# Two linear-attention layers: the key products of two jobs made by the same matmuls

## The chip, the cores and the metric

The kernel runs on one core of a Trainium2 chip. The metric is the device time of one execution in microseconds; the time before is the median of three runs. The profiled execution is a further one, and its time and its span are given below.

## The reference

The input x has 32 sequences of 128 tokens with 512 features, in float32. Two layers follow each other, with 16 heads in the first and 8 in the second; each is, for one sequence (`mask`, `cond`, weights and biases given):

```
xn = layernorm(x) * s + b
q, k, v = xn @ Wq + bq, xn @ Wk + bk, xn @ Wv + bv      # 512 x 512 each
k[masked tokens] = -inf (layer 0) or -1e6 (layer 1);  v[masked tokens] = 0
q = softmax(q, over the features of a head)
k = softmax(k, over the 128 tokens)
y = q @ (k.T @ v)                                       # head by head
h = layernorm(y) * (1 + scale(cond)) + shift(cond)      # FiLM, from silu(cond) @ We
x = x + silu(h) @ Wo + bo
```

## The kernel before

**Jobs.** Two sequences are a job; 16 jobs in a layer make 32 jobs, 0 to 31. `job()` writes out a job's operations: load and normalise (z), transpose by DVE and a round trip over DRAM (`zb`, `zd`), scale into `xnT` (features on partitions) on ACT, keys, q and v, softmaxes, attention (`pa`, `py`), second norm, transposes (`yb`, `yd`) and Silu into `hT`, output products (`oa` to `oe`), and the store. Job 0 (`plain`) multiplies directly. The last job transposes on TensorE (`xtp`, `htp`) and makes its output products (`op`) directly too, storing four pieces of 128 KB; every other job stores 512 KB at once.

**Seven products.** In jobs 1 to 31 the product of (2 sequences) x (2 halves of the features) with (2 x 2 quarters of a weight) is made of seven products of blocks in place of eight. `sums()` makes four sums of token blocks on POOL (`Sx`, L615), `sum_w` those of the weights. For the keys the stationary operand is a quarter of the weight and the moving one a block of tokens, so that a matmul moves 128 columns (one sequence); for q, v and the output the tokens are stationary, and 512 or 256 columns move. A float32 matmul leaves two records in the profile. A product of the keys is four matmuls, eight records (L743). The first product of a PSUM bank is copied out with the bias by ACT (`kcopy`, L749), two later products are added into the same bank, and the other banks are added in SBUF by DVE (`kadd`, L754):

```python
kprod(1, Ak); kcopy(0, 0); kprod(2, Bk); kadd(0, 0, Bk)
kprod(6, Ak, False); kcopy(0, 1); kprod(4, Ck)
...
```

After that the mask is added on POOL (L788), the maximum taken on DVE (L791), exp on ACT (L795), the keys of layer 0 scaled on POOL (L800), and transposed.

**Buffers.** `xnT`, `Sx` and `kT` have two buffers of a job each. All eight PSUM banks are shared. The film weights `we` have one buffer; a film group is 16 small matmuls (`em`, L546) behind a load of 1 MB.

**Order.** Each operation is recorded with `op(place, engine, estimated time, function, reads, writes, due=...)`. A planner (`Plan.schedule`) then lists them: at each step it takes the engine that can start first and, on it, the operation with the earliest due time. The due time is the job's base (31 us a job) plus the `due` of the call plus an entry of the table `SHIFT`, which holds a shift for each place and stage; `LATER` does this for loads, and `SAFE` is a margin for results of another engine. Each engine runs its list in order and waits on semaphores.

## Time and profile before

| | us |
|---|---|
| median of 3 runs (lowest, highest) | 915.11 (914.37, 915.85) |
| profiled execution, own time | 916.37 |
| its span on the core | 914.6 |
| TensorE (PE) busy in the span | 900.1 |
| VectorE (DVE) busy | 775.1 |
| ScalarE (ACT) busy | 625.2 |
| GpSimd (POOL) busy | 530.9 |

Busy times of matmuls overlap a little, so that what a matmul costs is read from the distance between the starts of two that follow each other. In a line of the timeline stand start, length, engine, line of the code, operation, output and inputs, shape and number; what ended an idle stretch before it is in brackets. In a line of a stretch the length comes first, then the busy time and number of instructions of PE, its weight loads, DVE, ACT and POOL, the granted clock, the share of DMA and its rate.

### The profile page before, as it was taken

How to read it: one execution, taken by the hardware profiler on the slowest of the kernel's cores; microseconds unless marked ns; L12 is line 12 of the kernel's file. 1: busy time of each engine (PE TensorE's matmuls, PEld its weight loads, DVE VectorE, ACT ScalarE, POOL GpSimd, SP SyncE). 2: the span in 40 equal slices, each digit the busy share in tenths (PEclk: the TensorE clock that was granted, in tenths of full speed). 3: DMA queues.
4: the chain of work that ended last, by engine and by line, in shares of the span. 5: the costliest groups of instructions: out<-in, count | busy, mean ns of one | idle time of the engine just before them, and what ended most of it. 6: DMA issues, size and time to landing. Idle time of an engine off the chain costs nothing.

```text
span 914.6 us, 18770 instructions
## 1 busy us (share of the span) xinstructions
PE 900.1 (98%) x6438; PEld 638.7 (70%) x6438; DVE 775.1 (85%) x1628; ACT 625.2 (68%) x1562; POOL 530.9 (58%) x737
## 2 busy tenths in 40 slices
PE   6999999999999999999999999999999999999998
PEld 2657567777776777766776866776777776776766
DVE  4778998879797898889999799898988997889775
ACT  3544857777867778588496757887478776666853
POOL 2465637677745778567555564654556664466543
PEclk9999999999999999999999999999999999999999
DMA  7588989595888676887969758656868465665742
GB/s 223 164 251 241 275 244 316 179 281 184 243 272 251 192 258 211 258 254 216 288 207 275 218 159 260 200 199 205 253 211 258 163 212 194 214 190 173 225 144 93
DMA packets 129891, 202.50 MB, mean 221 GB/s; under 512 B 13699, under 2 KB 81539, under 8 KB 129797
## 3 DMA queue, kind: packets, MB, share of 16 engines
q1 hardware_dynamic: 129796, 201.31, 71.0%
q8 instruction: 51, 0.84, 0.4%
q14 instruction: 44, 0.35, 0.1%
HBM read 120.00 MB, written 81.26 MB: 220 GB/s over the span
## 4 chain that ended last, share of the span: by engine, by line
PE 95%; DMA 3%; ACT 1%; DVE 1%; SPq 0%; issue 0%; ACTq 0%
PE bank_qa L817 17%; PE bank_qe L817 11%; PE bank_ka L743 9%; PE bank_oa L1013 9%; PE bank_py L946 6%; PE bank_ke L743 6%; PE bank_oe L1013 6%; PE bank_qc L817 6%; PE bank_qb L817 5%; PE bank_kc L743 3%; PE bank_oc L1013 3%; PE bank_ob L1013 3%; PE bank_kb L743 3%; PE bank_pa L925 3%; PE bank_qp L832 2%; DMA we<-in_We_dram 2%
## 5 line engine op out<-in xcount | busy, mean ns | idle before, releaser
L795 ACT ACTIVATE kT<-kT,kmax 128x128 f32<-128x128 f32 x256 | 99.8, 391 | 54.6 <-DVE kmax L791 52.5
L858 POOL TENSOR_TENSOR q<-q,qmax 128x512 f32<-128x512 f32 x64 | 67.1, 1051 | 118.1 <-DVE qmax L857 115.2
L749 ACT ACTIVATE kT<-bank_ka,cols_c 128x128 f32<-128x128 f32 x248 | 76.6, 362 | 86.2 <-PE bank_ka L743 84.5
L788 POOL TENSOR_TENSOR kT<-kT,mb 128x512 f32<-128x512 f32 x64 | 81.9, 1280 | 71.7 <-DVE kT L754 55.4
L817 PE MATMUL bank_qa<-wqv,Sx 128*128 128x512 f32 x248 | 117.3, 595 | 1.6 <-DVE v L821 1.4
L817 PE MATMUL bank_qe<-wqv,Sx 128*128 128x512 f32 x248 | 116.8, 593 | 0.0
L977 ACT ACTIVATE hT<-yb,fc_c,fa_c 128x128 f32<-128x128 f32 x248 | 102.5, 483 | 0.4
L817 PEld LDWEIGHTS bank_qa<-wqv,Sx 128*128 128x128 f32 x248 | 44.6, 190 | 42.4 <-issue 36.6
L946 PEld LDWEIGHTS bank_py<-att_c,qT 128*128 128x128 f32 x512 | 64.4, 192 | 13.4 <-issue 11.1
L743 PEld LDWEIGHTS bank_ka<-Sx,wk 128*128 128x128 f32 x496 | 63.6, 192 | 14.3 <-issue 11.2
L615 POOL TENSOR_TENSOR Sx<-xnT 128x256 f32<-128x256 f32 x62 | 46.4, 757 | 46.1 <-PE bank_qe L817 23.9
L743 PEld LDWEIGHTS bank_ke<-Sx,wk 128*128 128x128 f32 x496 | 63.2, 192 | 12.7 <-issue 10.2
L817 PEld LDWEIGHTS bank_qe<-wqv,Sx 128*128 128x128 f32 x248 | 44.6, 190 | 39.1 <-issue 37.0
L695 ACT ACTIVATE xnT<-zb,cols_c 128x256 f32<-128x256 f32 x120 | 64.0, 591 | 6.5 <-PE bank_qc L817 6.5
L657 ACT ACTIVATE y<-y,nmrb,rstdb 128x512 f32<-128x512 f32 x60 | 47.0, 809 | 29.3 <-POOL nmrb L645 29.2
L946 PE MATMUL bank_py<-att_c,qT 128*128 128x128 f32 x512 | 66.2, 275 | 0.4 <-DVE att_c L934 0.4
L743 PE MATMUL bank_ka<-Sx,wk 128*128 128x128 f32 x496 | 65.9, 276 | 0.0
L743 PE MATMUL bank_ke<-Sx,wk 128*128 128x128 f32 x496 | 65.5, 276 | 0.0
L1013 PE MATMUL bank_oa<-wo,Sh 128*128 128x256 f32 x248 | 64.2, 382 | 0.1
L1013 PE MATMUL bank_oe<-wo,Sh 128*128 128x256 f32 x248 | 64.2, 382 | 0.0
L657 ACT ACTIVATE z<-z,nmra,rstda 128x512 f32<-128x512 f32 x60 | 47.0, 807 | 18.2 <-POOL nmra L645 17.6
L817 PE MATMUL bank_qc<-wqv,xnT 128*128 128x512 f32 x124 | 58.6, 595 | 0.0
(144 smaller groups left out, 2246.6 us busy)
## 6 DMA issues: line engine op xcount, KB each, us to landing
x<-x SPq DMA_DIRECT2D x32, 512.0 KB, 4.2
qd<-qb SPq DMA_DIRECT2D x31, 512.0 KB, 4.1
qb<-qd SPq DMA_DIRECT2D x124, 128.0 KB, 3.8
kd<-k SPq DMA_DIRECT2D x31, 512.0 KB, 4.3
k<-kd SPq DMA_DIRECT2D x124, 128.0 KB, 3.7
yd<-yb SPq DMA_DIRECT2D x31, 512.0 KB, 3.9
yb<-yd SPq DMA_DIRECT2D x124, 128.0 KB, 3.7
zd<-zb SPq DMA_DIRECT2D x30, 512.0 KB, 4.7
```

What stands on the lines that cost most here:

```text
L615: op(25, "POOL", pool(2 * T), lambda i=i, x=x, y=y, f=f: nc.gpsimd.tensor_tensor(S.ap[:, i], x(), y(), f), r, [(S, i)], due=due, lock=True)
L657: op(34, "ACT", act(512, 2, False), lambda: nc.scalar.activation(dst.ap[:, b, :], src.ap[:, b, :], AF.Identity, bias=nmr.ap[:, b : b + 1], ...
L695: op(39, "ACT", act(GT, 2, False), lambda c=c: nc.scalar.activation(xnT.ap[:, c, :].rearrange("p (b r t) -> p r b t", b=G, r=4), zb.ap[:, ...
L743: nc.tensor.matmul(t.ap[:, m * T : (m + 1) * T], kw[quarter].ap[:, c, m * P : (m + 1) * P], a()[:, c, :], start=(first and m == 0 and c == ...
L749: op(46, "ACT", act(T, 1), lambda m=m: nc.scalar.activation(kT.ap[:, 2 * h + m, i, :], Ak.ap[:, m * T : (m + 1) * T], AF.Identity, bias=co ...
L788: op(50, "POOL", pool(2 * GT), lambda hs_=hs_: nc.gpsimd.tensor_tensor(kT.ap[:, hs_].rearrange("p m b t -> p m (b t)"), kT.ap[:, hs_].rear ...
L795: op(52, "ACT", act(T, 1, False) + 0.093, lambda m=m, b=b: nc.scalar.activation(kT.ap[:, m, b, :], kT.ap[:, m, b, :], AF.Exp, bias=km.ap[: ...
L817: nc.tensor.matmul(t.ap, a()[:, c, :], wqv[quarter].ap[:, c, :], start=(first and c == 0), stop=(c == 1), skip_group_check=not first)
L858: op(61, "POOL", pool(512, False), lambda qh=qh, qm=qm: nc.gpsimd.tensor_tensor(qh(), qh(), qm.ap[:, :H].unsqueeze(2).to_broadcast([P, H, ...
L946: nc.tensor.matmul(py.ap[:, m * P : (m + 1) * P], qTc(b, m), att.ap[:, b, m, :], start=True, stop=True)
L977: op(81, "ACT", act(T, 2, False), lambda c=c, b=b: nc.scalar.activation(hT.ap[:, c, b * T : (b + 1) * T].rearrange("p (r t) -> p r t", r=4 ...
L1013: nc.tensor.matmul(t.ap[:, :hf], a()[:, c, :], ow[quarter].ap[:, c, :], start=(first and c == 0), stop=(c == 1), skip_group_check=not first)
```

## The change

The keys of two jobs (four sequences) are made by the same products. The jobs 2 and 3, 4 and 5, to 28 and 29 are 14 pairs; 1, 30 and 31 stay alone, and job 0 is as before. `job` becomes a generator that stops before the keys; a new function `keys` then records the key products for one job or two. A product of a pair still has four matmuls, and each moves 256 columns, two pieces of 128 that lie a slot apart. Tokens (`xnT`), token sums (`Sx`) and keys (`kT`) of two jobs lie in one tile each, with a slot for even and one for odd jobs, and are allocated once. A copy of ACT takes 256 columns and an addition of DVE 512 elements. Everything else of a job is as before.

The tables `SHIFT` and `LATER` are new throughout, and `SAFE` has other margins, so that the order of the instructions is another on every engine. In it, job 0's key products stand ahead of its q and v products, the first film groups come earlier, and at the end job 30's output products and its store come after job 31's. Loads of activation tables on ACT number 77, before 59.

```diff
-    SAFE = {"PE": 0.62, "DVE": 0.21, "ACT": 0.52, "POOL": 0.22, "SP": 4.38}
+    SAFE = {"PE": 0.77, "DVE": 0.16, "ACT": 0.55, "POOL": 0.30, "SP": 5.07}
...
-    k_xnT = kind("xnT", [P, NC, GT], 2)
-    k_S = {s: kind("S" + s, [P, 4, 2, T], 2) for s in "xh"}
-    k_kT = kind("kT", [P, NC, G, T], 2)
+    xnT2 = fixed("xnT", [P, NC, 2, GT])
+    Sx2 = fixed("Sx", [P, 4, 2, 2, T])
+    kT2 = fixed("kT", [P, NC, 2, G, T])
+    k_Sh = kind("Sh", [P, 4, 2, T], 2)
...
+    def keys(j, L, lefts):
+        n = f"{j}_{L}"
+        kw = W["k", L]
+        J = len(lefts)
+        at = slice(j % 2, j % 2 + J)
+        Ak, Bk, Ck, Ek = (bank.new(f"k{c}{n}") for c in "abce")
+        out_ = lambda t: t.ap[:, : J * GT].rearrange("p (m j t) -> p m j t", m=2, j=J)
...
+        def prod(i, t, first=True, due=5):
+            _, _, quarter, where = lefts[0][i]
+            made = [x for l in lefts for x in l[i][1]]
+            def moving(c):
+                if isinstance(where, tuple):
+                    return xnT2.ap[:, 2 * where[1] + c, at, where[0] * T : (where[0] + 1) * T]
+                return Sx2.ap[:, where, c, at]
+            def go():
+                for m in range(2):
+                    for c in range(2):
+                        nc.tensor.matmul(out_(t)[:, m], kw[quarter].ap[:, c, m * P : (m + 1) * P], moving(c),
+                                         start=(first and m == 0 and c == 0), stop=(c == 1), skip_group_check=True)
+            op(35, "PE", mm(4, J * T), go, made + [kw[quarter]], [t], due=due)
+        def copy(i, h, due=5):
+            for m in range(2):
+                op(36, "ACT", act(J * T, 1), lambda m=m: nc.scalar.activation(
+                    kT2.ap[:, 2 * h + m, at, i, :], out_(Ak)[:, m], AF.Identity, bias=col(L, C_BK + 2 * h + m)),
+                    [Ak, cols_sb], parts(i, h, [m]), due=due)
+        def add(i, h, t, due=6):
+            op(37, "DVE", dve(J * GT), lambda: nc.vector.tensor_tensor(
+                kT2.ap[:, 2 * h : 2 * h + 2, at, i, :], kT2.ap[:, 2 * h : 2 * h + 2, at, i, :], out_(t), ALU.add),
+                [t], parts(i, h, range(2)), due=due)
...
-        kT, km, ks = k_kT.new(n), k_km.new(n), k_ks.new(n)
+        km, ks = k_km.new(n), k_ks.new(n)
+        kT = lambda: kT2.ap[:, :, slot]
+        yield left
...
+    FIRST = [i for i in range(2, 2 * B // G - 2, 2)]
+    jobs, lefts = {}, {}
...
-        job(j, L, FAR(i), i in (0, 2 * B // G - 1), i == 0)
+        jobs[i] = job(j, L, FAR(i), i in (0, 2 * B // G - 1), i == 0)
+        lefts[i] = next(jobs[i])
+        if i in FIRST:
+            continue
+        pair = [i - 1, i] if i - 1 in FIRST else [i]
+        plan.base = pair[0] * STEP
+        if i:
+            keys(pair[0] % (B // G), L, [lefts[q] for q in pair])
+        for q in pair:
+            plan.base = q * STEP
+            for _ in jobs[q]:
+                pass
```

## The prediction

> **What bounds the kernel now.** I read the page first, then the stretches, then single matmuls.

> ```profile
> PE 900.1 (98%) x6438; PEld 638.7 (70%) x6438; DVE 775.1 (85%) x1628; ACT 625.2 (68%) x1562; POOL 530.9 (58%) x737
> ...
> PEclk9999999999999999999999999999999999999999
> ...
> PE 95%; DMA 3%; ACT 1%; DVE 1%; SPq 0%; issue 0%; ACTq 0%
> ```

> TensorE is busy nearly all the time at full clock, and the chain that ended last is made of its matmuls. The stretches say where it is not:

> ```profile
> 115.00:450.00 335.00, 335.00 (x2496) 240.33 (x2495) 291.97 (x622) 246.38 (x615) 215.12 (x298) 1.00 0.78 242
> 450.00:850.00 400.00, 400.00 (x2851) 287.69 (x2850) 354.41 (x747) 280.96 (x701) 226.20 (x313) 1.00 0.68 213
> ```

> The first figure after the length is PE: 335.00 of 335 and 400.00 of 400 us. In the middle 735 us only less matmul time can help. The timeline of PE gives the price of a matmul as the distance between starts (durations overlap):

> ```profile
> 306.36 1.03 PE L1013 MATMUL bank_oa<-wo,hT 128*128 128x256 f32 x4
> 307.22 1.03 PE L1013 MATMUL bank_oc<-wo,hT 128*128 128x256 f32 x4
> ...
> 319.37 1.05 PE L743 MATMUL bank_ke<-Sx,wk 128*128 128x128 f32 x8
> 320.26 1.06 PE L743 MATMUL bank_kc<-xnT,wk 128*128 128x128 f32 x8
> 321.15 1.06 PE L743 MATMUL bank_kb<-xnT,wk 128*128 128x128 f32 x8
> 322.05 1.88 PE L817 MATMUL bank_qe<-wqv,Sx 128*128 128x512 f32 x4
> ```

> A key product (8 records of 128 columns) takes 0.895 us, 111.9 ns a record; four records of 256 columns take 0.86 us, 215.5 ns a record. The ends are where PE waits:

> ```profile
> 16.55 9.30 PE L832 MATMUL bank_qp<-wqv,xnT 128*128 128x512 f32 x16 [1.03 <-ACT xnT L712]
> 25.68 7.07 PE L763 MATMUL bank_kp<-xnT,wk 128*128 128x256 f32 x32
> ...
> 65.23 1.98 PE L817 MATMUL bank_qb<-wqv,xnT 128*128 128x512 f32 x4
> 68.43 1.08 PE L546 MATMUL bank_em<-we,cT_c 128*32 128x128 f32 x32 [1.22 <-DMA we<-in_We_dram]
> ```

> ```profile
> 108.44 1.43 PE L743 MATMUL bank_kc<-xnT,wk 128*128 128x128 f32 x8 [0.70 <-ACT xnT L695]
> ```

> ```profile
> 895.03 1.13 PE L946 MATMUL bank_py<-att_c,qT 128*128 128x128 f32 x8 [0.39 <-DVE att_c L934]
> ...
> 896.87 1.05 PE L946 MATMUL bank_py<-att_c,qT 128*128 128x128 f32 x8
> ...
> 901.38 0.66 PE L966 MATMUL bank_htp<-ident_c,y 128*128 128x128 f32 x4
> ```

> ```profile
> 911.34 0.48 DVE L998 SCALAR_TENSOR_TENSOR x<-x,nanf_c,bank_op 128x256 f32<-128x256 f32 x1 [1.25 <-PE bank_op L995]
> ```

> ```profile
> we<-in_We_dram SPq DMA_DIRECT2D x8, 1024.0 KB, 7.2
> ...
> out_dram<-x SPq DMA_DIRECT2D x15, 512.0 KB, 3.6
> ...
> out_dram<-x SPq DMA_DIRECT2D x4, 128.0 KB, 1.8
> ```

> **Part 1, the key products.** 14 pairs (jobs 2 to 29) make 98 products of 8 records with 256 columns, at 8 x 0.2155 = 1.724 us, in place of 196 at 0.895. Each pair of products gives 2 x 0.895 - 1.724 = 0.066 us, in all 98 x 0.066 = **-6.5 us**. Jobs 1, 30 and 31 stay single. [...] The rows say 2 x 111.9 - 215.5 = 8.3 ns a record, and I take the rows. No row shows a moving operand of two pieces of 128 columns; from below nothing, from above the two 128-column records' own time (gain 0). I take the contiguous price, as the 256-column rows of L763 and L1013 agree (25.68 to 32.59 is 32 x 0.216).

> **Part 2, copies and adds.** ACT: 224 copies of 128 columns (L749, 362 ns mean) become 112 of 256 (L766 does that form in 474): -28 us busy. DVE: 112 adds at 0.41 become 56 of 512 columns, for which L824 takes 0.68: -8 us. The new order carries 77 table loads for 59: 18 x 1.283 = +23 us on ACT. [...]

> **Part 3, waits in the middle.** xnT, Sx and kT become single tiles of two slots. The waits that the new program carries are by slot and part, so a write to one slot doesn't wait for a reader of the other. New is that the pair's first key product waits for the second job's tokens. I summed PE's work, by the rows above, between the last product that reads a slot's old tokens and the first that needs its new ones, where four ACT writes of 0.59 must fit: for second jobs 2.6 us at the least (pair 22/23), then 6.9, median 14; before, the least was 2.6 as well (four jobs of 32), median 11, without a stall. From the last q/v product to the job's first attention product: least 3.5, median 20 (before 1.8 and 10). From a product to the next into the same q bank: least 0.86, then 1.72, against 0.0 and 1.0 before, where the wait of 1.40 near 104 us sits. So the new order is looser, and I charge 0.

> **Part 4, the head.** Before: 1.03 at 16.55; 16 records of 0.43 took 9.13 instead of 6.88, so 2.25; 1.5 before 68.43; about 3.3 from 102 to 109 (1.40, 0.70 and what surrounds them): 8.1 us lost. After: the key matmuls of job 0 stand first (6.9 us from about 15.5, weights loaded early), then Q's 6.9 to 29.3: 3.3 us won. But the first film group (`em`) and a q product now follow. That product needs job 1's tokens, whose ACT writes stand behind the exp of q: q add 0.7, max 0.7, subtraction 1.05, exp 0.63 after 29.3, then the writes: 33.2; PE waits 2.6. The film weights have one buffer: the second load starts when the first group ends (31), takes 7.2, and one product of 1.72 us covers it: PE waits 3.3, to 38.5. In all 5.9 for 8.1: **-2.2**, and I use -2.

> **Part 5, the tail.** Job 31 is the last, and its chain from py through the norm to `htp` (transposes), Silu and `op` (output products) has no work of its own to hide it. Before, four groups of job 30's output products fill PE between the second py and the first `htp` (897.8 to 901.38), and PE does not wait. In the new order both `htp` groups stand right behind py, and job 30's output products come after them. From the end of the first py (before: 896.16): y 0.65, stats 0.65, another add 0.4, aggregate 0.15, POOL 0.25+0.6, the norm 0.55 with the second y and stats ahead of it on DVE: first `htp` 4.0, second 5.0 after py, where the order leaves 1.8; then four Silus of 0.36 before the first `op`. PE loses 3.0 there. Behind it 0.2 (Silus of job 30) and 0.5 (the last product waits for an add), 3.7 in all where before lost 0.5: +3.2. A v add stuck behind eight exps on DVE's queue holds PE 1.6 before that, against 1.2: +0.4. Last comes job 30's output: one DMA of 512 KB (3.6) instead of 128 KB (1.8): +1.8. Sum **+5.4**.

> **The sum.** -6.5 - 2 + 5.4 = -3.1 against the profiled execution: span 914.6, own time 916.37, so 913.3. The median of the runs lies 1.26 lower (915.11): 912.0. The measurement can tell about 0.2%, 1.8 us, from no change.

> **Rivals.**
> A, the sum above: 912.0, 909.5 to 914. For it: a full PE and unchanged matmuls. Chance 0.50.
> B, the tail costs little, since DVE and ACT come earlier than I string them up: -6.5 - 2 + 1.8 = -6.7, 908.4 (906 to 909.5). Against it: the `htp` groups stand where they stand. 0.15.
> [...]
> D, slower: the pair's first key product waits for the second job's tokens. The row at 108.44 is that wait, 0.70. Once for each pair: 14 x 0.7 = 9.8, 921.8. It decides from 3.1 / 14 = 0.22 us a pair, and is measurably slower from 0.35 (917). For it: the keys of two jobs come in one burst, so ACT, which must write the tokens, gets eight copies and 16 exps close together. Against it: the median of 14 us. 0.20, the lower prices likelier.

> **Numbers.** Faster by over 0.2% (below 913.3): 0.45 of A and all of B: 0.60. Within: 0.05 of A, 0.13 of C, 0.04 of D: 0.22. Slower (above 916.9): 0.02 of C, 0.16 of D: 0.18. The range 907.0 to 918.0 leaves out the best of B and the dear part of D; A and B alone hold 906.5 to 914.

> **What would show it.** Right: the pair's products start 1.72 us apart where nothing stands between; PE 735 of 735 us in the middle; gaps before the second film group near 33 to 38 us and before `htp` and the first `op`, some 3 us each; the last DMA is 512 KB. Wrong: a pair product at 1.79 or more (C); a wait on ACT's xnT before L683 in most pairs (D); no gap at `htp` (B).

## The result, and the profile after

| | before | after |
|---|---|---|
| median, us | 914.99 (914.37 to 915.85, 4 runs) | 931.05 (929.87 to 931.89, 4 runs) |
| profiled execution, own time | 916.37 (shown above) | 931.89 |
| its span | 914.6 | 930.1 |

The change makes the kernel slower by 16.1 us: the ratio is 1.0174, with a 95% interval from 1.0156 to 1.0192. The forecast was 912.0, from 907 to 918.

The page of the changed kernel, with the same parts as shown before:

```profile
PE 902.0 (97%) x5654; PEld 614.3 (66%) x5654; DVE 769.0 (83%) x1572; ACT 630.7 (68%) x1468; POOL 537.5 (58%) x737
...
PEclk9999999999999999999999999999999999999997
...
PE 88%; DVE 5%; ACT 2%; DMA 2%; issue 1%; SPq 1%; POOL 0%; ACTq 0%; POOLq 0%
```

PE has fewer records (5654, before 6438), and its share of the chain that ended last fell from 95% to 88%. The stretches say where it lost; first the two ends of the kernel before, then the changed kernel:

```profile
0.00:115.00 115.00, 104.30 (x690) 64.69 (x691) 85.56 (x172) 61.13 (x164) 59.05 (x87) 1.00 0.79 232
850.00:915.00 65.00, 60.77 (x407) 46.00 (x405) 43.14 (x91) 36.70 (x83) 30.54 (x40) 1.00 0.44 143
```

```profile
0.00:115.00 115.00, 101.26 (x620) 60.67 (x621) 78.19 (x151) 49.11 (x121) 52.06 (x74) 0.97 0.78 240
115.00:450.00 335.00, 330.10 (x2056) 223.66 (x2055) 285.14 (x597) 254.97 (x596) 218.05 (x301) 1.00 0.77 232
450.00:850.00 400.00, 398.43 (x2539) 276.64 (x2538) 354.02 (x717) 289.33 (x671) 234.48 (x322) 1.00 0.70 216
850.00:931.00 81.00, 72.16 (x443) 53.38 (x441) 51.64 (x109) 37.34 (x83) 32.92 (x43) 0.94 0.40 133
```

The middle from 450 us on is nearly full. The two ends are not, and the granted clock (the figure behind POOL) is 0.97 and 0.94 there, where the kernel before shows 1.00. PE's timeline at the first end:

```profile
16.08 8.93 PE L802 MATMUL bank_kp<-xnT_c,wk 128*128 128x256 f32 x32
24.84 7.03 PE L854 MATMUL bank_qp<-wqv,xnT_c 128*128 128x512 f32 x16
31.80 1.08 PE L547 MATMUL bank_em<-we,cT_c 128*32 128x128 f32 x32
35.66 3.02 PE L839 MATMUL bank_qb<-wqv,xnT_c 128*128 128x512 f32 x4 [2.77 <-ACT xnT_c L751]
38.61 1.80 PE L547 MATMUL bank_em<-we,cT_c 128*32 128x128 f32 x32
40.34 1.98 PE L839 MATMUL bank_qa<-wqv,xnT_c 128*128 128x512 f32 x4
...
83.27 2.53 PE L839 MATMUL bank_qe<-wqv,Sx_c 128*128 128x512 f32 x4 [2.70 <-DVE v L846]
85.59 3.05 PE L683 MATMUL bank_ka<-xnT_c,wk 128*128 128x256 f32 x8
88.47 1.88 PE L839 MATMUL bank_qb<-wqv,xnT_c 128*128 128x512 f32 x4
...
91.92 1.89 PE L683 MATMUL bank_kc<-xnT_c,wk 128*128 128x256 f32 x8
93.64 1.89 PE L683 MATMUL bank_ka<-Sx_c,wk 128*128 128x256 f32 x8
95.37 1.89 PE L683 MATMUL bank_kb<-xnT_c,wk 128*128 128x256 f32 x8
...
119.48 1.13 PE L839 MATMUL bank_qa<-wqv,xnT_c 128*128 128x512 f32 x2 [2.58 <-ACT xnT_c L751]
```

Two things are to be read. The products of a pair start 1.72 us apart (91.92, 93.64, 95.37), as forecast. And behind the waits of 2.77 and 2.70 us PE works at a lower pace: the q product at 35.66 takes 2.95 us to the next start where 1.72 is its price, the film group 1.73 for 1.01, the pair product at 85.59 2.88. The granted clock is 0.84 from 30 to 40 us, 0.83 from 80 to 90 and 0.59 from 906 to 912. The tail:

```profile
904.01 1.05 PE L968 MATMUL bank_py<-att_c,qT 128*128 128x128 f32 x8
907.23 1.12 PE L988 MATMUL bank_htp<-ident_c,y 128*128 128x128 f32 x4 [2.16 <-DVE y L653]
908.65 1.09 PE L988 MATMUL bank_htp<-ident_c,y 128*128 128x128 f32 x4 [0.30 <-DVE y L653]
909.67 2.08 PE L1017 MATMUL bank_op<-wk_o,hT 128*128 128x256 f32 x4
911.54 3.95 PE L1017 MATMUL bank_op<-wo,hT 128*128 128x256 f32 x12
915.33 1.03 PE L1038 MATMUL bank_ob<-wo,hT 128*128 128x256 f32 x4
```

The 16 records of `op` take 5.66 us from 909.67 to 915.33; at 0.2155 us each they are worth 3.45.

**Where the time went.** For each job I took the start of its first `pa` and subtracted the work that stands before it in PE's list, at the prices of the rows (0.430, 0.2155 and 0.112 us a record). What is left is time lost on PE. At job 3 it is 153.45 - 125.1 = 28.4 us after and 137.38 - 120.5 = 16.9 before: the head lost 11.45 us more. By job 29 (844.64 us) 2.34 more were lost, 1.6 of them in two waits of 0.58 and 0.99, and by job 31 another 0.81. From job 31's `pa` to the end of the span it took 30.6 us (899.48 to 930.1), before 22.5 (892.09 to 914.6), with 0.86 us more work there: 7.25. Together 21.85 lost, and PE's list is worth 6.35 us less (881.03 for 887.38): 15.5, the difference of the spans. The prices are rounded, which can move the 2.34 and the 6.35 by some 0.3 us each, in opposite directions. Of the 11.45, 0.6 is the first wait of all, for `rows`: 6.80 us here and 6.16 before. In other traces whose order has the same head it was 6.28 and 5.7 (first and second trial of the fill) and 5.9 us (trial of the tail).

### The profile page after: what moved, and what is told of

Read it like the earlier page. It is cut to its first block, busy times and chain, and to the rows that moved or that the text cites. A ratio compares the mean times of both kernels' runs of the same rounds, so it can differ in the third digit from the quotient of the medians.

```text
span 930.1 us, 17033 instructions
## 1 busy us (share of the span) xinstructions
PE 902.0 (97%) x5654; PEld 614.3 (66%) x5654; DVE 769.0 (83%) x1572; ACT 630.7 (68%) x1468; POOL 537.5 (58%) x737
## 4 chain that ended last, share of the span: by engine, by line
PE 88%; DVE 5%; ACT 2%; DMA 2%; issue 1%; SPq 1%; POOL 0%; ACTq 0%; POOLq 0%
PE bank_qa L839 16%; PE bank_qe L839 11%; PE bank_oa L1038 8%; PE bank_ka L683 8%; PE bank_py L968 5%; PE bank_oe L1038 5%; PE bank_ke L683 5%; PE bank_qb L839 5%; PE bank_qc L839 5%; PE bank_pa L947 3%; PE bank_kb L683 3%; PE bank_ob L1038 3%; PE bank_oc L1038 3%; PE bank_kc L683 3%; PE bank_qp L854 1%
## 5 line engine op out<-in xcount | busy, mean ns | idle before, releaser
L818 ACT ACTIVATE kT_c<-kT_c,kmax 128x128 f32<-128x128 f32 x256 | 100.2, 393 | 39.3 <-DVE kmax L814 38.7
L839 PE MATMUL bank_qe<-wqv,Sx_c 128*128 128x512 f32 x248 | 117.6, 597 | 3.7 <-DVE v L846 2.7
L839 PE MATMUL bank_qa<-wqv,Sx_c 128*128 128x512 f32 x248 | 117.1, 594 | 1.8 <-DVE v L843 1.8
L689 ACT ACTIVATE kT_c<-bank_ka,cols_c 128x256 f32<-128x256 f32 (+1 forms) x136 | 53.1, 453 | 87.1 <-PE bank_ka L683 76.1
L811 POOL TENSOR_TENSOR kT_c<-kT_c,mb 128x512 f32<-128x512 f32 x64 | 82.2, 1292 | 50.4 <-DVE kT_c L694 33.2
L751 ACT ACTIVATE xnT_c<-zb,cols_c 128x256 f32<-128x256 f32 x120 | 65.2, 595 | 8.4 <-PE bank_qc L839 5.0
L839 PE MATMUL bank_qb<-wqv,xnT_c 128*128 128x512 f32 x124 | 59.5, 602 | 2.8 <-ACT xnT_c L751 2.8
L839 PE MATMUL bank_qa<-wqv,xnT_c 128*128 128x512 f32 x124 | 58.7, 595 | 3.2 <-ACT xnT_c L751 3.2
L683 PE MATMUL bank_ka<-Sx_c,wk 128*128 128x256 f32 (+1 forms) x272 | 60.0, 363 | 0.0
L683 PE MATMUL bank_ke<-Sx_c,wk 128*128 128x256 f32 (+1 forms) x272 | 59.6, 362 | 0.0
## 6 DMA issues: line engine op xcount, KB each, us to landing
x<-x SPq DMA_DIRECT2D x32, 512.0 KB, 4.5
kd<-k SPq DMA_DIRECT2D x31, 512.0 KB, 4.0
qd<-qb SPq DMA_DIRECT2D x31, 512.0 KB, 4.3
k<-kd SPq DMA_DIRECT2D x124, 128.0 KB, 4.1
qb<-qd SPq DMA_DIRECT2D x124, 128.0 KB, 4.1
yd<-yb SPq DMA_DIRECT2D x31, 512.0 KB, 4.2
yb<-yd SPq DMA_DIRECT2D x124, 128.0 KB, 3.7
zd<-zb SPq DMA_DIRECT2D x30, 512.0 KB, 5.2
```

What stands on the lines that cost most here:

```text
L683: nc.tensor.matmul(out_(t)[:, m], kw[quarter].ap[:, c, m * P : (m + 1) * P], moving(c), start=(first and m == 0 and c == 0), stop=(c == 1) ...
L689: op(36, "ACT", act(J * T, 1), lambda m=m: nc.scalar.activation(kT2.ap[:, 2 * h + m, at, i, :], out_(Ak)[:, m], AF.Identity, bias=col(L, C ...
L751: op(42, "ACT", act(GT, 2, False), lambda c=c: nc.scalar.activation(xn(c).rearrange("p (b r t) -> p r b t", b=G, r=4), zb.ap[:, :, :, c, : ...
L811: op(50, "POOL", pool(2 * GT), lambda hs_=hs_: nc.gpsimd.tensor_tensor(kT()[:, hs_].rearrange("p m b t -> p m (b t)"), kT()[:, hs_].rearra ...
L818: op(52, "ACT", act(T, 1, False) + 0.093, lambda m=m, b=b: nc.scalar.activation(kT()[:, m, b, :], kT()[:, m, b, :], AF.Exp, bias=km.ap[:, ...
L839: nc.tensor.matmul(t.ap, a()[:, c, :], wqv[quarter].ap[:, c, :], start=(first and c == 0), stop=(c == 1), skip_group_check=not first)
```

## The experiments

**1. The pairs' products split again.** Everything else, the order too, stays.

```diff
-    nc.tensor.matmul(out_(t)[:, m], kw[quarter].ap[...], moving(c), start=(...), ...)
+    for o in range(J):
+        nc.tensor.matmul(out_(t)[:, m, o], kw[quarter].ap[...], moving(c)[:, o], start=(... and o == 0), ...)
```

> Each key product of a pair is issued as two products of 128 columns again, back to back, in the same place of the same order; copies, adds, tiles and order stay those of the changed kernel (931.05). Theory (Part 1 of the prediction held, the loss lies elsewhere): 98 products get dearer by 0.066 us each, so +6.5 us, 937.5 (936 to 938.5). Rival (the 256-column product of two pieces brings nothing): 931 +- 1. Rival (the pair's long product is itself what other engines wait for): below 930.

Measured: 936.45 us (ratio 1.0226, 1.0208 to 1.0244), 5.4 us over the changed kernel; the span grew by 5.3. In its timeline 16 records of 128 columns stand where 8 of 256 stood, 1.79 us from start to start:

```profile
91.44 1.95 PE L684 MATMUL bank_kc<-xnT_c,wk 128*128 128x128 f32 x16
93.23 1.95 PE L684 MATMUL bank_ka<-Sx_c,wk 128*128 128x128 f32 x16
```

The longer products do pay on PE, and are not what made the kernel slow. What pairs ask of the order is not tested by this.

**2. The waits filled with idle matmuls.** This asks whether the low pace comes from the waits. Three bursts of matmuls on the identity stand ahead of the three products that waited longest.

```diff
+            if o.fill:
+                for _ in range(o.fill[0]):
+                    self.nc.tensor.matmul(o.fill[1].ap[:, :P], self.warm.ap, self.warm.ap, start=True, stop=True)
             o.fn()
```

> 68 idle matmuls of 128 columns are added, in three bursts (24, 24, 20: about 2.7, 2.7 and 2.2 us), where PE waited 2.77 us (near 35.7), 2.70 us (near 83.3) and 2.16 us (near 907.2) in the changed kernel; they write a PSUM bank that the next product overwrites, and nothing waits for them. The waits themselves stay. Theory (after such a wait the granted clock is half for some us, which made the work behind it 1.2 + 0.7, 0.6 + 1.2 and 1.0 + 1.2 us longer): the clock stays 1.00 in these stretches and the time falls by 4 to 6 us, to 925 to 927. Rival (the drop of the clock has nothing to do with the idle time): 931 or up to 1 us more, and the clock falls at the same places.

Measured: 932.84 us, 1.8 over the changed kernel and not the 4 to 6 under it that were expected. The clock stayed at 1.00 at all three places, but each burst was about twice as long as its wait (5.62, 5.62 and 4.63 us for 2.77, 2.70 and 2.16). The q product came at 37.48 for 35.66, yet the second one behind it at 40.31 for 40.34: full clock paid for the overrun. The trial was repeated at half the size.

> The three bursts of idle matmuls again, at half their number (12, 12, 10). In the first trial each of them took two records of 112 ns, so a burst was 5.5 and 4.5 us long, overran its wait by 2 to 3 us, and the full clock behind it only paid for that. Now 2.7, 2.7 and 2.2 us. Theory: clock 1.00 in the three stretches, 4 to 6 us under the changed kernel's 931, so 925 to 927. Rival (full clock gains nothing, since the next wait takes it): 930 to 932.

Measured: 927.48 us (ratio 1.0130, 1.0104 to 1.0156), 3.6 us under the changed kernel, with the time of the three waits still there, now filled. Its stretches 30 to 40, 80 to 90 and 906 to 912 us, where the changed kernel has clocks of 0.84, 0.83 and 0.59:

```profile
30.00:40.00 10.00, 9.52 (x99) 5.92 (x98) 7.79 (x15) 5.34 (x16) 6.83 (x8) 1.00 0.57 195
80.00:90.00 10.00, 10.00 (x70) 7.51 (x60) 8.73 (x17) 6.61 (x12) 6.65 (x11) 1.00 1.00 333
906.00:912.00 6.00, 5.24 (x27) 4.14 (x25) 0.55 (x1) 5.57 (x15) 0.99 (x2) 1.00 0.28 87
```

It is less than the 4 to 6 expected, and two rows say why: the clock now fell at another place, behind the wait near 120 us (0.89 from 110 to 125 us, where the changed kernel has 1.00), and the film groups, which the low clock had delayed, now wait for their weights (1.6 us in two waits).

**3. A series of waits by itself.** Behind the end of the kernel stand 18 bursts with waits of growing length between them: nine from 0.55 to 3.32 us, then the first eight of these again.

```diff
         plan.emit()
+        for i, n in enumerate(2 * list(range(9))):
+            b = ps.tile([P, 512], F32, tag="bank", name=f"gap{i}", bufs=8)
+            for m in range(10 if i < 9 else 13):
+                nc.tensor.matmul(b, ident.ap, u, start=True, stop=True)
+            nc.scalar.copy(w[:, :P], b[:, :P])
+            for m in range(n):
+                nc.scalar.copy(w[:, P : 2 * P], w[:, :P])
+            nc.scalar.copy(u[:, :P], w[:, P : 2 * P])
```

> Behind the last output of the changed kernel stands a series of its own: 18 bursts of matmuls (10 of 512 columns, then 13 in the second half), and between two bursts PE waits for a chain of copies on ACT, of 2 to 10 links, so for some 1 to 4 us. About 250 us are added; the time means nothing. Theory (the clock falls for a wait above some length): bursts behind short waits start at 0.215 us for 256 columns' worth (0.43 a record of 512) and those behind waits longer than a threshold between 2.2 and 2.7 us at about half that pace, always. Rival (the clock follows the load of a fixed window of time): near the threshold the two halves of the series differ, as the wait falls differently into the window.

A burst of 20 records lasts 8.85 us at full clock. Five bursts of the first half of the series, then the last of the second half (26 records, 11.43 us at full clock):

```profile
964.49 8.85 PE L1114 MATMUL gap<-xnT_c,ident_c 128*128 128x512 f32 x20 [1.67 <-ACT xnT_c L1118]
975.35 10.55 PE L1114 MATMUL gap<-xnT_c,ident_c 128*128 128x512 f32 x20 [2.00 <-ACT xnT_c L1118]
988.23 8.85 PE L1114 MATMUL gap<-xnT_c,ident_c 128*128 128x512 f32 x20 [2.33 <-ACT xnT_c L1118]
999.74 10.55 PE L1114 MATMUL gap<-xnT_c,ident_c 128*128 128x512 f32 x20 [2.66 <-ACT xnT_c L1118]
1013.27 10.55 PE L1114 MATMUL gap<-xnT_c,ident_c 128*128 128x512 f32 x20 [2.99 <-ACT xnT_c L1118]
...
1134.86 11.43 PE L1114 MATMUL gap<-xnT_c,ident_c 128*128 128x512 f32 x26 [2.99 <-ACT xnT_c L1118]
```

A wait of 2.00 us brought the low clock and one of 2.33 did not; those of 2.00, 2.66 and 2.99 did in the first half and did not in the second. So in this series the length does not decide alone: the two halves differ at the same lengths, as the rival said. Each time it happened, the burst was 1.7 us longer. Waits up to 1.67 us never brought it in this series.

Where the wait falls in time goes with it. In the changed kernel's trace the clock changes at 19.66, 36.73, 40.14, 84.51, 87.92, 907.12, 913.95 and 927.60 us; the distances from the first (17.07, 20.48, 64.85, 68.26, 887.46, 894.29 and 907.94 us) are 5, 6, 19, 20, 260, 262 and 266 times 3.413 us. In the kernel before there is one change, 894.29 us behind the first record, 262 times as much. The series, cut into stretches of this length, shows behind the waits of 2.00 and 2.33 us:

```profile
972.72:976.13 3.41, 1.41 (x4) 0.49 (x3) 0.00 (x0) 1.75 (x6) 0.00 (x0) 1.00 0.00 0
976.13:979.55 3.42, 3.42 (x5) 1.35 (x4) 0.00 (x0) 0.00 (x0) 0.00 (x0) 0.50 0.00 0
986.37:989.79 3.42, 1.56 (x4) 0.85 (x5) 0.00 (x0) 1.64 (x6) 0.00 (x0) 1.00 0.00 0
989.79:993.20 3.41, 3.41 (x9) 1.50 (x9) 0.00 (x0) 0.00 (x0) 0.00 (x0) 1.00 0.00 0
```

With 1.41 us of busy PE in the first stretch the next was at half clock, with 1.56 us at full clock. In the changed kernel, cut in the same way, half clock followed the stretches with 1.07, 1.24 and 1.36 us of busy PE (from 33.31, 81.10 and 903.71 us). The wait of 2.58 us at 119.48 is split there between two stretches with 1.67 and 1.94 us, and the clock stayed. That the busy time of such a stretch decides is my reading of these rows.

**4. Head and tail of the order, one at a time.** The operations are those of the changed kernel; their list is written out.

```diff
+ORDER = [
...
+]
     def emit(self):
-        for o in self.schedule():
+        for o in [self.ops[i] for i in ORDER]:
```

`ORDER` starts as the planner's own list. A search moved single operations among those of their engine, only in the named stretch, and kept a move where engines that run their lists in order would end earlier at the planner's durations.

> The changed kernel with the same operations, but with another order of those that stood in the first 150 us (jobs 0 to 4, loads, film); from there on every engine has the order of the changed kernel. Theory (the loss of the head is a matter of the order alone, and not of the pairs): PE's waits of 2.77, 2.70, 2.58 us and what surrounds them go, with the half clock behind them, and the time falls by 12 to 19 us, to 912 to 919. Rival (pairs themselves: the first pair needs the tokens of job 3 a job earlier, whatever the order): at most 4 us, 927 or more.

Measured: 911.23 us (ratio 0.9947, 0.9932 to 0.9962): 20 us, and already under the kernel before. With the pairs, the tiles and the middle unchanged, the first two stretches read:

```profile
0.00:115.00 115.00, 110.77 (x673) 67.28 (x674) 90.94 (x182) 62.76 (x160) 57.69 (x87) 1.00 0.85 269
115.00:450.00 335.00, 334.42 (x2078) 229.43 (x2077) 289.05 (x598) 253.34 (x581) 228.32 (x313) 1.00 0.79 237
```

Against the changed kernel PE has 9.5 + 4.3 = 13.8 us more busy time in them, and in the head it does not pay the 3.7 us of low clock (1.23 + 0.72 + 0.60 + 1.15, the excess of the rows at 35.66, 38.61, 83.27 and 85.59). Counted as above, job 3's first `pa` comes at 133.27 us for 153.45, with the same work before it: 20.2 us, about the whole gain of the medians. Not all of it undoes the change: 8.2 us are lost up to there, where the kernel before lost 16.9. Job 0's first products start at 11.81 us here, at 16.08 in the changed kernel and at 16.55 before.

The profiled execution of this trial (909.25 us) was faster than the other three (911.19 to 911.32). In it PE waited 2.16 us at `htp` as in the changed kernel, but without the low clock behind it; the others have a mean clock of 0.998 for its 1.000, which agrees with the low clock there.

> The changed kernel with another order of the operations that stood behind 850 us (jobs 27 to 31) and nothing else moved. Theory (tail lost 7.5 us against before, 2.8 of it half clock): 5 to 8 us less, 923 to 926. Rival (the tail is bound by job 31's chain in any order): less than 2 us, 929 or more.

Measured: 924.01 us (ratio 1.0099, 1.0079 to 1.0118), 7.0 less than the changed kernel. Work of job 30 stands between the two `htp` groups again:

```profile
902.45 0.66 PE L1189 MATMUL bank_htp<-ident_c,y 128*128 128x128 f32 x4
903.38 1.13 PE L1239 MATMUL bank_ob<-wo,hT 128*128 128x256 f32 x4 [0.28 <-ACT hT L1200]
904.35 1.03 PE L1239 MATMUL bank_oa<-wo,hT 128*128 128x256 f32 x4
906.26 0.66 PE L1189 MATMUL bank_htp<-ident_c,y 128*128 128x128 f32 x4 [0.88 <-DVE y L854]
```

**5. Both ends.** First by a search over both stretches together, and the same for the kernel with single keys.

> Head and tail of the changed kernel's order both set anew (a search over both together), the middle from 150 to 850 us as it was. Theory (the loss is the order of the two ends): the sum of the two single changes, 931 - 20 - 7 = 904 (902 to 906), under both kernels. Rival (a better head only moves the wait to the middle or the tail): 908 or more.

> The kernel before (single keys) with the order of its two ends set anew by the same search and the middle as it was: what pairs are worth at equal care for the order. Theory (pairs save 6.5 us of products, and the rest is order): 6 us above the pairs with both ends set anew, about 910. Rival (pairs bring nothing once the order is as good, since their keys come in bursts): the same as with pairs, within 2 us.

Measured: 909.57 with pairs (0.9939, 0.9915 to 0.9963), 907.55 with single keys (0.9916, 0.9898 to 0.9933). Both missed. Single keys were 2.0 us faster, where 6 us slower had been expected: the rival's case, though their orders are not the same. The pairs missed 904: this search had ended in another head, where film groups wait, and in another tail, where `htp` waits almost as long as in the changed kernel. PE's waits of it:

```profile
PE bank_htp L1188 <- DVE y L853: 2.5, 2, 1.8
PE bank_em L747 <- DMA we<-in_We_dram: 2.1, 2, 1.7
```

So the head of one trial and the tail of the other were put together exactly, and the split of trial 1 was made in that kernel too.

> Exactly the two single changes together: the head of the one trial (911.2) and the tail of the other (924.0), the middle of the changed kernel's order. The earlier kernel with both ends set anew (909.6) had a different head, in which PE waits 2.1 us for the film weights, and a different tail, in which it waits 2.5 us at htp. Theory (the ends are separate): 931 - 20 - 7 = 904 (903 to 906). Rival (ends are not separate, a better head is lost again in the tail): 908 to 911, as in that kernel.

> The kernel with both single changes, each pair product issued as two products of 128 columns in the same place. Theory (where PE is full the products' 6.5 us count in full; with the changed kernel's order 5.3 us of them showed): 5 to 6.5 us over that kernel, 910. Rival (a good order has slack that hides it): under 2 us.

Measured: 905.60 us with pairs (ratio 0.9890, 0.9877 to 0.9904), the fastest kernel here, 9.9 us under the kernel before. It misses 904 by 1.6, and the cause of that is not shown. One candidate: in the trace of the tail trial job 3's first `pa` comes 1.34 us earlier than in the changed kernel's, though nothing was changed there, so that not all of its 7.0 us need be the tail. Its waits:

```profile
PE bank_qe L1040 <- DVE att_c L1157: 1.0, 1, 1.0
PE bank_htp L1189 <- DVE y L854: 0.9, 1, 0.9
PE bank_qc L1040 <- DVE x L1249: 0.6, 1, 0.6
```

Split, it takes 911.56 (0.9956, 0.9943 to 0.9970): in this order the pairs are worth 6.0 us.

**6. The whole order.** The search over all jobs, for pairs and for single keys.

> Pairs, with the order of all jobs set anew, the middle too (where 2.1 us of waits stood at four places). Theory: the waits of the middle go as well, 902 (900 to 905). Rival (a search over a model of the engines gains nothing more on the chip): 904 or more.

> Single keys (the kernel before), with the order of all jobs set anew in the same way as for the pairs: the comparison at equal care. Theory (a pair is worth its products, 6.5 us): about 6 us over the pairs so treated, 906 to 909. Rival (the pairs' demands on the head eat that): within 2 us of them.

Measured: 908.73 with pairs (0.9922, 0.9908 to 0.9935) and 913.70 with single keys (0.9977, 0.9964 to 0.9989). Both missed (900 to 905 and 906 to 909 were expected); the pairs are 5.0 us faster, but neither beats the best of its kind. With pairs the middle did become full (335.00 of 335 and 400.00 of 400 us), but the tail waits 2.3 us at `htp` again; with single keys the middle lost (333.88 and 396.67). The comparison that these trials were for is therefore not made: best against best, 905.60 with pairs stands against 907.55 with single keys, and the intervals of their ratios overlap. That pairs are worth 6.0 us within one order is shown; that the best order with them beats the best order without them is open.

## Why the prediction was wrong, by its steps

**Part 1 (-6.5) held.** 1.72 us from product to product, 5.4 us shown by the split in the changed order and 6.0 in the good one. That is 6.9 and 7.6 ns for each of the 784 records, so the price from the rows (8.3 ns) was a little high. Rival C, with little or no gain from the longer products (chance 0.15), is out: no run shows the smaller gain that it counted with, and the splits showed 5.4 and 6.0 us.

**Part 2 (0 in the sum) is not contradicted.** ACT is busy for 630.7 us of 930.1 (68%), where the part's terms give 625.2 - 28 + 23 = 620.2 of 912.0 (68%), and behind job 3 PE waits for it only once, 0.2 us.

**Part 3 (0 in the middle) was nearly right.** 2.3 us were lost from job 3 to job 29 where none was charged. Rival D, one wait for tokens for each of 14 pairs, did not happen in the middle. Its mechanism came once, in the head and at another product. The 2.58 us at 119.48 are a q product of job 4 that waits for job 4's tokens, and ACT writes them in between the exps of the first pair:

```profile
115.85 1.28 ACT L818 ACT_TABLE_LOAD   x1
117.15 0.40 ACT L818 ACTIVATE kT_c<-kT_c,kmax 128x128 f32<-128x128 f32 x1
...
118.84 0.59 ACT L751 ACTIVATE xnT_c<-zb,cols_c 128x256 f32<-128x256 f32 x1
...
119.71 0.59 ACT L751 ACTIVATE xnT_c<-zb,cols_c 128x256 f32<-128x256 f32 x1
...
120.59 1.09 ACT L751 ACTIVATE xnT_c<-zb,cols_c 128x256 f32<-128x256 f32 x2
```

Part 3 measured distances in PE's work alone. It did not add up what stood in ACT's queue between the same two points, and from 110 to 125 us ACT was busy for 14.89 us of 15.

**Part 4 (-2) is the step that failed.** It set 5.9 us of loss after against 8.1 before. But the 8.1 reach to 109 us, and of the new order only the first 40 us were followed, to the second film group. Up to there its sizes were off, but not its sum. Of the 3.3 us won, 2.25 were the slow pace of the first products before; it came again, as job 0's key products took 8.76 us (16.08 to 24.84) for 6.9. So Q ended at 31.8 and not at 29.3. The wait for job 1's tokens, forecast at 2.6, measured 2.77. The wait of 3.3 for the film weights was not there: the tokens came at 35.66 and not at 33.2, and the low clock covered the rest, which the second trial of the fill, at full clock, shows as 0.48 us. With 1.95 of low clock, 2.77 + 1.86 + 1.95 = 6.6 us were lost up to there, for the 5.9. The failure is what stands behind 40 us. Not forecast at all were the 2.70 at 83.27 (a v addition that stands behind norms and transposes on DVE), between 110 and 127 us 0.67, 0.80, 2.58, 0.63 and 0.84, and another 0.84 at 141. The head lost 11.45 us more than before, not 2 less. The trial with another head shows that the order decides this: with the same pairs it lost 8.2 us to job 3, not 28.4.

**Part 5 (+5.4) had the right mechanism.** The first `htp` waits, and job 30's products come too late to fill PE. It measured 7.3 behind job 31's `pa`, and 0.8 between jobs 29 and 31; 2.2 of the 7.3 are the low clock on `op`. The waits themselves were close to their sizes: 2.16 + 0.30 at `htp` and 0.61 at the last product, for 3.0 and 0.5.

**A term that no part had** is the low clock behind waits. Its rows add up to 3.7 us in the head and 2.2 in the tail; filling the waits brought back 3.6 net. The prediction read PEclk of 9 in all slices before and took a steady clock for granted, though its own rows held the 2.25 us at the start, at half pace, and though it forecast waits of 2.6 to 3.3 us where the kernel before had none over 1.4 us behind its start.

With the measured terms the sum is -6.35 + 11.45 + 2.34 + 0.81 + 7.25 = +15.5 between the two spans, where the prediction had -3.1.

## What to carry to other kernels

When a change brings a new order, walk the new order on every engine's queue to the same point for before and after, above all at the start and the end, where nothing hides a wait; a sum that follows one side to 109 us and the other to 40 us compares nothing. Test a step by keeping all the rest in place: a split product at the same position and an order with one end exchanged told in two runs what the whole change could not. And a wait of the matmul engine can cost twice, once as the wait and once for the pace behind it: in the series a wait of 2.00 us made the burst behind it 1.70 us longer, while one of 2.33 us did not.

## What the runs showed of the hardware

At the start of both kernels the clock column says 1.00, but the traces have no record of the clock up to 20.93 us (kernel before) and 19.66 us (changed kernel). Up to there job 0's first products run at half pace: before, records of 512 columns start 0.85 us apart from 17.56 to 20.12 us and 0.43 from 20.96 on; in the changed kernel, records of 256 columns start 0.427 us apart from 16.67 to 19.66 and 0.216 behind 19.88.

Matmuls that nobody needs held the clock at 1.00 in all three places. Bursts of 2.94, 2.94 and 2.40 us, about as long as the waits, brought 3.6 us; at twice the length (5.62, 5.62 and 4.63 us) the gain was gone (1.8 us over the changed kernel).
